# A four-layer graph kernel: counts and tables issued straight behind the lookups, and fp8 stores held to their place in SyncE's queue

## The chip, the cores and the metric

The kernel runs on one NeuronCore of a Trainium2 chip. The metric is the device time in microseconds, the median of several runs. Engines are called TensorE (PE in the profile; its weight loads are PEld), VectorE (DVE), ScalarE (ACT), GpSimd (POOL) and SyncE (SP, which only issues DMAs; its queue is SPq). Each engine works through its own instructions in the order in which they are written down, and the engines wait for each other through semaphores.

## What is computed

There are 16 graphs of 1024 nodes with 128 features each; `adj` holds 0 or 1. Four layers follow each other, each added to its input and normalised:

```python
# layer 0: masked attention over the neighbours
x = layernorm(x + softmax(masked(relu_q @ relu_k.T, adj)) @ relu_v)
# layer 1: for each node the maximum over its neighbours, feature by feature
x = layernorm(x + max_j(relu(p[i] + q[j] + b) * adj[i, j]))
# layer 2: sum over neighbours, then two dense products
x = layernorm(x + where(nodemask, relu(((1 + eps) * x + x_agg) @ W1 + b1) @ W2 + b2, 0))
# layer 3: some edges are removed row after row, each row depending on earlier ones
# ("dilation"); then three rounds of mean over neighbours, dense products, batch norm
x = layernorm(x + graph_sage(x, dilate(adj)))
```

The removal of edges (`_dilate_pattern`) is sequential in the row: the removals of a row also clear the column.

## The kernel before

Most of the time is one stage, `layers_012`, in which layers 0 to 2 and the removal of edges run side by side. Its backbone is the maximum of layer 1. The nodes of a graph are taken in groups of six; for each group a table holds the maxima over all 64 subsets. Two groups make a slot, so a graph has NP = 86 slots, and 16 graphs make 1376. A slot has two half slots `h`, one for each half of the 1024 columns. In a half slot:

- `look_up` (L843) writes `pg` in PSUM with four matmuls: the table's part `high` and its part `low`, each for two groups, times `hot`, a matrix that has a one where a column's subset is the table's. There are two `pg` buffers.
- `count` (L812, L813) prepares `hot` for the slot after the next: a matmul of the fp8 tile `AT` with the constant `lit` into `pm`, and ScalarE's activation of `pm` into `hot`.
- `table` (L824, L827), in every second slot, transposes the tables of two slots ahead on TensorE into `pt` and copies them on ScalarE into `high`; `low_part` (L832, L834), half a slot later, subtracts `high` from `pt` by a matmul and copies the rest into `low`. `pm` and `pt` share two PSUM buffers.
- VectorE takes the maximum of `best` and `pg` into `best` (L908).

All other work of the stage is written as generators ("streams"): attention of the next graph (`scores` with `off` L337 and the exponentials `e` L359; `attend` with the transposes of `e` L387, their copy `eT` L390, the product `pav` L397), the rest of layers 1 and 2 (`rest`), the tables' subset maxima on VectorE (`tables_of`, `sub` L482 and L486) and layer norm. A stream hands over one piece at a time with an engine and an estimated cost. A planner, `advance`, issues in each half slot those pieces for which its budgets (`ROOM`) and its delays allow it, TensorE's first and then the others; mostly a piece that needs another's result is issued half a slot later. The removal of edges is a further generator, `dilation`, asked by `dilate_on` when its due time has come. It works in 32 blocks of 32 rows, one block in about 43 slots. In each, GpSimd goes through 31 steps (L669 to L679), in which it issues what comes due there; VectorE prepares the next block (`prepare`, with the scan `U` L544, its result `V` passed through DRAM, L555 and L556); `hit` goes through DRAM to VectorE (L686, L689, `hit_T` L703); and `remove` ranks edges with TensorE and ScalarE (`pturn` L590, `prank` L599, `rank` L601), finds the edges `gone` on VectorE (L613, two buffers) and stores them from SyncE (L615).

In the half slot the order of issue is: lookups, a piece of `dilation` (before or after the streams), the streams' pieces, `low_part`, `count`, `table`, and last VectorE's maximum. TensorE, ScalarE, VectorE and GpSimd keep this order as written (`manual_schedule`). SyncE isn't among them: the order of its DMAs is made by the scheduler, from its own estimate of when each is ready.

`load_columns` brings in the adjacency. In each graph nine chunks of 120 rows of the transposed adjacency are loaded, by a DMA that GpSimd issues (L764) and that converts to fp8, into `AT`, which has four buffers. The call for chunk `at` also stores chunk `at - 1` from SyncE (L758) into `adj8` in DRAM, which layer 3 reads much later. It is called every ten slots, two chunks ahead of use. SyncE's queue also has the loads of X (L747), the stores of layer 2's result (L466) and all DMAs of the removal of edges that are named above, except for the loads of `E`, `An` and `AT`, which GpSimd issues.

After the stage, from about 5088 us, layer 3 runs: three rounds over 16 graphs with other code, which is not touched here.

Of the kernel before, what the change touches and what calls it, by code (L numbers as in the profile page):

```python
# [39 lines left out]
B, N, D, H2 = 16, 1024, 128, 256  # L40
P = 128
T = N // P
GS = 6
PS = 2 * GS
PC = 10
CH = PC * PS
# [28 lines left out]
def tile_graph_layers(ctx: ExitStack, tc, a, out):  # L75
    nc = tc.nc
# [95 lines left out]
    for b in range(B):  # L172
        q, g = divmod(b, G)
        nc.gpsimd.dma_start(out=half_rows[g * R:(g + 1) * R, :, q],
                            in_=a["nodemask"][b].rearrange("(k r) -> r k", r=R))
# [21 lines left out]
    adj8 = [dram.tile([N, N], F8, name=f"adj8_{b}") for b in range(B)]  # L197
# [39 lines left out]
    def behind(ins, start):  # L237
        for i in nc.cur_bb.bb.instructions[start:]:
            tc.add_manual_dep(i, ins.name, mybir.DependencyInfo(
                mybir.DependencyClass.NoSync, mybir.DependencyReason.SCHED_ONLY), reason="pace")  # L240

    def layers_012():
# [227 lines left out]
        def tables_of(b):  # L470

            if b:
                yield ask("V", 0, urgent=True, after=("tables", b - 1))
            for g0 in range(0, NP, TG):
                n_g = 2 * min(TG, NP - g0)
                yield ask("V", 0.01, same=True, urgent=True, after=("q", b))
                made.append((b, g0))
                yield ask("V", 0.1, same=True, urgent=True, after=("used", *made[-3]) if len(made) > 2 else None)
                qg = qs[b].rearrange("o (g s) -> o g s", s=GS)
                subs[b, g0] = w2.tile([P, TG, P], F32, name="sub", bufs=2)  # L480
                sub = subs[b, g0].rearrange("o t (a s) -> o (t a) s", a=2)
                nc.vector.memset(sub[:, :n_g, 0:1], LOWEST)  # L482
                for k in range(GS):
                    n = 1 << k
                    yield ask("V", 0.06 + n * n_g / 960, same=(n < 8), urgent=True)
                    nc.vector.tensor_max(sub[:, :n_g, n:2 * n], sub[:, :n_g, 0:n],  # L486
                                         qg[:, 2 * g0:2 * g0 + n_g, k:k + 1].to_broadcast([P, n_g, n]))
                happened["sub", b, g0] = now
            happened["tables", b] = now
# [255 lines left out]
        def load_x(b):  # L745
            X[b] = apool.tile([P, T, D], F32, name="X", bufs=3)
            nc.sync.dma_start(out=X[b], in_=x[b].rearrange("(t p) d -> p t d", p=P))  # L747
# [4 lines left out]

        def load_columns(at):
            b, c = divmod(at, T + 1)
            if at:
                before, k = divmod(at - 1, T + 1)
                rows = min(CH, N - k * CH)
                nc.sync.dma_start(out=adj8[before][k * CH:k * CH + rows], in_=AT[at - 1][:rows])  # L758
            if b < B:
                rows = min(CH, N - c * CH)  # L760
                t = AT[at] = apool.tile([CH, N], F8, name="AT", bufs=4)
                if rows < CH:
                    nc.gpsimd.memset(t, 0.0)
                nc.gpsimd.dma_start(out=t[:rows], in_=adjT[b, c * CH:c * CH + rows])  # L764

        An, AT, subs, qs, ps, values, exps, bests, hots, tables = ({} for _ in range(10))
# [8 lines left out]
        def start(stream, first=False):  # L775
            pending[stream] = [next(stream, None), -9]
            streams.insert(0 if first else len(streams), stream)
# [27 lines left out]
        def count(s, h):  # L805

            b, g = divmod(s, NP)
            c, r = divmod(g, PC)
            if h == 0:
                hots[s] = w2.tile([P, N], F32R, name="hot", bufs=3)  # L810
            pm = psum.tile([P, 512], F32, tag="subset", name="pm", bufs=2)
            nc.tensor.matmul(pm, lit[:, r, :], AT[b * (T + 1) + c][:, halves[h]], start=True, stop=True)  # L812
            nc.scalar.activation(hots[s][:, halves[h]], pm, AF.Relu, bias=one_less)  # L813

        def table(s):

            b, g = divmod(s, NP)
            g0 = g - g % TG
            assert ("sub", b, g0) in happened, (s, [(x.__name__, pending[x]) for x in streams], room)
            pt = psum.tile([P, 512], F32, tag="subset", name="pt", bufs=2)[:, :2 * P]  # L820
            if g + 2 - g0 == min(TG, NP - g0):
                happened["used", b, g0] = now
            for k in range(2):
                nc.tensor.matmul(pt[:, k * P:(k + 1) * P], subs[b, g0][:, g - g0 + k, :], ident, is_transpose=True,  # L824
                                 start=(k == 0), stop=(k == 1))
            high = w2.tile([P, 2 * P], F32R, name="high", bufs=2)
            nc.scalar.copy(high, pt)  # L827
            tables[s] = pt, high

        def low_part(s):  # L830
            pt, high = tables[s]
            nc.tensor.matmul(pt, less, high, start=False, stop=True, skip_group_check=True)  # L832
            low = w2.tile([P, 2 * P], F32R, name="low", bufs=2)
            nc.scalar.copy(low, pt)  # L834
            tables[s] = high, low

        def look_up(s, h, pg):

            at = s % 2
            for k, part in enumerate(tables[s - at]):  # L840
                for a in range(2):
                    rows = slice(64 * a, 64 * a + 64)
                    nc.tensor.matmul(pg[:, a], part[rows, at * P:(at + 1) * P], hots[s][rows, halves[h]],  # L843
                                     start=(k == 0), stop=(k == 1))

        def merge(b, h):
            best, s = bests[b], halves[h]
            nc.vector.tensor_max(best[:, 0, s], best[:, 0, s], best[:, 1, s])
# [5 lines left out]
        def dilate_on():  # L854
            nonlocal due, wants_bank
            if due <= now and not (wants_bank and taken >= 2 and given.get(taken - 2, 1e9) > now):
                after, cost, wants_bank = next(dilate, (B * NP, 0, False))
                due += after
                room["V"] -= cost

        def slot(s, last):

            nonlocal now
            now = s
            b, g = divmod(s, NP)
            if s >= 0 and g == 0:
                bests[b] = bests[b - 1] if b else w4.tile([P, 2, N], F32, name="best")
                if b + 1 < B:
                    start(tables_of(b + 1), True)
                    load_x(b + 1)  # L870
                    start(attend(b + 1))
                    start(scores(b + 1))
            if s >= 0 and g % PC == 0 and b * (T + 1) + g // PC + 2 <= B * (T + 1):
                load_columns(b * (T + 1) + g // PC + 2)
            for h in range(2):
                now = s + 0.5 * h
                for e in ROOM:
                    room[e] = min(room[e] + ROOM[e] / 2, ROOM[e] / (2 if e in ("PE", "V") else 1))
                if s >= 0:
                    pg = psum.tile([P, 2, 512], F32, tag="wide", name="pg", bufs=2)  # L880
                    look_up(s, h, pg)
                early = s >= 0 and due < now
                if early:
                    dilate_on()
                advance(("PE",))
                advance(("A", "V", "Pool"))
                if s >= 0 and not early:
                    dilate_on()
                if h == 0 and s % 2 and s + 1 < last:
                    low_part(s + 1)  # L890
                if s + 2 < last:
                    count(s + 2, h)
                    if h and s % 2 == 0:
                        table(s + 2)
                if s >= 0:
                    own = bests[b][:, :, halves[h]]
                    if g == 0:
                        if b:
                            if h:
                                merge(b - 1, h)  # L900
                            total(b - 1, h)
                        nc.vector.tensor_copy(own, pg)
                        if b and h:
                            start(rest(b - 1))
                    else:
                        if g == NP - 1 and h:
                            merge(b, 0)
                        nc.vector.tensor_max(own, own, pg)  # L908
            if s >= 0:
                hots.pop(s)  # L910
# [4 lines left out]
        for at in range(2):  # L915
            load_columns(at)
# [13 lines left out]
        with tc.manual_schedule(engines={mybir.EngineType.PE, mybir.EngineType.Activation, mybir.EngineType.DVE,  # L930
# [13 lines left out]
            last = rest(B - 1)  # L944
# [426 lines left out]
```

## Time and profile before

| what | value |
|---|---|
| median of 3 runs | 6208.64 us (6201.9 to 6210.01) |
| the profiled execution's own time | 6199.75 us |
| its span, first to last instruction | 6198.0 us |
| mean granted TensorE clock | 0.962 |
| busy in the span: TensorE, VectorE, ScalarE, GpSimd | 90%, 79%, 64%, 58% |
| TensorE busy in 142 to 5088 us (the slots) | 4486.93 of 4946 us |
| VectorE, ScalarE, GpSimd busy in the same | 4253.75, 3360.82, 3390.78 us |
| TensorE busy from 5088 us to the end | 1015.75 of 1110 us |

In the lines of the profile, a group of instructions is named by line, engine and operation, then what it writes and what it reads, the shape, and how often it ran; behind the bar stand its total busy time and the mean of one in ns; behind the second bar the time that the engine stood idle before it, and what ended most of that. A line of waits gives who waited for whom, the total in us, how often, and the longest. A line of the timeline gives the start in us, the duration, engine, line and operation, and in brackets the idle time before it with what ended it.

### The profile page before, as it was taken

Reading aid. Unit: us, or ns where it says so; the run is one execution under the profiler, and the core shown is the slowest. Engines: PE = TensorE matmul, PEld = TensorE weight load, DVE = VectorE, ACT = ScalarE, POOL = GpSimd, SP = SyncE. Lnnn points to the kernel's source line nnn. Section 1 sums busy time; section 2 is a strip of 40 time slices with the busy share of each in tenths; the row PEclk is TensorE's granted clock in tenths of the full one; section 3 lists DMA queues with packets and bytes.
Section 4 is the critical chain, followed back from the end, with each engine's and each line's share of the span. In section 5 each row is a group of like instructions: output and inputs, shape, how many; then the busy total and the mean of one; then the engine's idle time right before and its main releaser. Section 6 shows DMA issues by size and latency. Waiting matters only on the chain.

```text
span 6198.0 us, 93287 instructions
## 1 busy us (share of the span) xinstructions
PE 5582.7 (90%) x30144; PEld 3046.0 (49%) x30250; DVE 4870.0 (79%) x7484; ACT 3988.2 (64%) x7362; POOL 3613.1 (58%) x11879
## 2 busy tenths in 40 slices
PE   5989899989898989999989798989999878999998
PEld 4545454545454545454545454545444435555654
DVE  3888788888888888889888788888889875555455
ACT  3767676767676767677767576767666554344855
POOL 2676666667666767677777757667677651110114
PEclk8999999989999999999999899999999989999999
DMA  5021213121212212122121211212121014554645
GB/s 42 11 33 25 40 22 42 22 40 24 40 24 31 32 32 32 32 32 38 26 43 22 39 24 31 31 31 33 31 33 28 19 41 124 159 144 133 214 163 191
DMA packets 496976, 334.28 MB, mean 54 GB/s; under 512 B 303338, under 2 KB 448228, under 8 KB 492388
## 3 DMA queue, kind: packets, MB, share of 16 engines
q1 hardware_dynamic: 405504, 260.29, 14.5%
q0 software_dynamic: 89008, 67.42, 12.6%
q8 instruction: 237, 3.88, 0.3%
q14 instruction: 255, 2.09, 0.1%
q10 hardware_dynamic: 1972, 0.59, 0.1%
HBM read 362.38 MB, written 133.96 MB: 80 GB/s over the span
## 4 chain that ended last, share of the span: by engine, by line
PE 31%; DVE 10%; ACT 4%; POOL 3%; issue 2%; DMA 1%; SPq 0%; DVEq 0%; POOLq 0%; ACTq 0%
PE pg L843 7%; PE pagg L1071 5%; DVE best L908 5%; PE pm L812 3%; PE po L1101 2%; PE po L1095 1%; PE pa L439 1%; PE pav L397 1%; PE pp L300 1%; ACT hot L813 1%; PE pdeg L1026 1%; DVE near L1014 1%; PE psc L349 1%; PE prank L599 1%; PE pe L387 1%
## 5 line engine op out<-in xcount | busy, mean ns | idle before, releaser
L908 DVE TENSOR_TENSOR best<-best,pg 128x1024 f32<-128x1024 f32 x2720 | 3259.3, 1214 | 512.6 <-PE pg L843 501.7
L813 ACT ACTIVATE hot<-pm,one_less 128x512 fp32r<-128x512 f32 x2752 | 1887.4, 689 | 780.5 <-PE pm L812 773.2
L843 PE MATMUL pg<-hot,high 64*128 64x512 f32 x5504 | 1407.3, 508 | 258.9 <-DVE best L908 220.8
L843 PE MATMUL pg<-hot,low 64*128 64x512 f32 x5504 | 1115.5, 402 | 0.0
L812 PE MATMUL pm<-AT,lit 120*128 120x512 fp8e4 x2752 | 1085.9, 395 | 4.5 <-ACT low L834 3.5
L843 PEld LDWEIGHTS pg<-hot,high 64*128 64x128 f32 x5504 | 523.5, 187 | 1014.6 <-DVE best L908 492.8
L669 POOL TENSOR_SCALAR sc<-low_counts,half_mask,rest 16x1 f32<-16x1 f32 x992 | 354.4, 357 | 393.9 <-DVE rest L655 283.2
L843 PEld LDWEIGHTS pg<-hot,low 64*128 64x128 f32 x5504 | 537.9, 192 | 0.0
L812 PEld LDWEIGHTS <-lit 120*128 120x128 fp8e4 x2752 | 270.3, 98 | 389.8 <-issue 313.5
L674 POOL TENSOR_SCALAR sc<-sc 16x1 f32<-16x1 f32 x992 | 393.1, 396 | 105.1
L834 ACT CAST low<-pt 128x256 fp32r<-128x256 f32 x688 | 256.0, 372 | 263.3 <-PE pt L832 261.9
L671 POOL TENSOR_SCALAR sc<-sc 16x1 f32<-16x1 f32 x992 | 324.5, 327 | 107.6
L1116 POOL TENSOR_TENSOR length<-length,mhalf 128x8 f32<-128x8 f32 x48 | 78.9, 1644 | 489.2 <-DVE length L1115 489.2
L676 POOL TENSOR_SCALAR hit<-V,sc 16x31 bf16<-16x31 bf16 (+30 forms) x992 | 362.4, 365 | 0.0
L677 POOL TENSOR_SCALAR last_rank<-V,sc 16x31 f32<-16x31 bf16 (+30 forms) x992 | 342.9, 346 | 0.0
L832 PE MATMUL pt<-high,less 128*128 128x256 f32 x688 | 279.2, 406 | 67.6 <-ACT high L827 61.5
L824 PE MATMUL pt<-ident,sub 128*128 128x128 f32 x1376 | 277.5, 283 | 51.8 <-ACT hot L813 50.0
L486 DVE TENSOR_TENSOR sub<-sub,q 128x24 f32<-128x24 f32 (+11 forms) x768 | 304.0, 397 | 24.8 <-ACT q L304 10.4
L397 PE MATMUL pav<-v,eT 128*128 128x128 f32 x2048 | 301.5, 292 | 2.0 <-ACT eT L390 2.0
L397 PEld LDWEIGHTS pav<-v,eT 128*128 128x128 f32 x2048 | 255.4, 196 | 73.3 <-issue 55.7
L670 POOL TENSOR_SCALAR sc<-sc 16x1 f32<-16x1 f32 x992 | 237.0, 239 | 86.5
L349 PE MATMUL psc<-kT,qT 128*128 128x256 f32 x1024 | 276.3, 388 | 9.9 <-issue 9.9
(270 smaller groups left out, 9662.9 us busy)
## 6 DMA issues: line engine op xcount, KB each, us to landing
removed<-gone SPq DMA_DIRECT2D x128, 256.0 KB
An<-in_adj_dram POOLq DMA_DIRECT2D x16, 1024.0 KB, 16.0
E<-in_adj_dram POOLq DMA_DIRECT2D x128, 128.0 KB, 6.6
gone_all<-removed POOLq DMA_DIRECT2D x64, 256.0 KB, 10.2
near<-adj SPq DMA_DIRECT2D x16, 1024.0 KB
kept<-near SPq DMA_DIRECT2D x16, 1024.0 KB
share<-share SPq DMA_DIRECT2D x32, 512.0 KB
hidden<-r SPq DMA_DIRECT2D x32, 512.0 KB
```

Of the source, the lines that this page charges most:

```text
L349: nc.tensor.matmul(psc[:, 256 * i:256 * (i + 1)], qT[:, t * P:(t + 1) * P], kT[:, s.start + 256 * i:s.start + 256 * (i + 1)], start=False, ...
L397: nc.tensor.matmul(pav, eT[:, c, :], values[b][:, c, :], start=(c == 0), stop=(c == T - 1))
L669: gp.tensor_scalar(half, mine, half_mask[:, m], rest[:, n:n + 1], op0=ALU.mult, op1=ALU.add)
L671: gp.tensor_scalar(sf, half, 5.5, sf, op0=ALU.is_gt, op1=ALU.mult)
L674: gp.tensor_scalar(to, at, sf, none, op0=ALU.subtract, op1=ALU.subtract)
L676: gp.tensor_scalar(hit[:, n, n + 1:], V[:, n, n + 1:], at, None, op0=ALU.is_equal)
L677: gp.tensor_scalar(last[:, n + 1:], V[:, n, n + 1:], to, None, op0=ALU.is_le)
L812: nc.tensor.matmul(pm, lit[:, r, :], AT[b * (T + 1) + c][:, halves[h]], start=True, stop=True)
L813: nc.scalar.activation(hots[s][:, halves[h]], pm, AF.Relu, bias=one_less)
L843: nc.tensor.matmul(pg[:, a], part[rows, at * P:(at + 1) * P], hots[s][rows, halves[h]], start=(k == 0), stop=(k == 1))
L908: nc.vector.tensor_max(own, own, pg)
L1071: nc.tensor.matmul(pa[:, s], piece[:, t, :], m[c][:, s], start=(i == 0), stop=(i == 15))
```

## The change

Two edits are made in `slot` and `load_columns`.

In a half slot `low_part`, `count` and `table` are now issued directly behind `look_up`, ahead of `dilation`'s piece and of the streams' pieces. The planner's decisions are the same, and so is VectorE's maximum at the end of the half slot.

The call of `load_columns` for chunk `at` now stores chunk `at - 2`, and the store is given a dependency for the scheduler alone (no semaphore), which ties it behind the instruction written just before it. `behind` is a helper that was there already. One more call, at slot 80 of the last graph, makes the last store.

```diff
         def load_columns(at):
             b, c = divmod(at, T + 1)
-            if at:
-                before, k = divmod(at - 1, T + 1)
+            if at > 1:
+                before, k = divmod(at - 2, T + 1)
                 rows = min(CH, N - k * CH)
-                nc.sync.dma_start(out=adj8[before][k * CH:k * CH + rows], in_=AT[at - 1][:rows])
+                begin = len(nc.cur_bb.bb.instructions)
+                nc.sync.dma_start(out=adj8[before][k * CH:k * CH + rows], in_=AT[at - 2][:rows])
+                behind(nc.cur_bb.bb.instructions[begin - 1], begin)
...
-            if s >= 0 and g % PC == 0 and b * (T + 1) + g // PC + 2 <= B * (T + 1):
+            if s >= 0 and g % PC == 0:
                 load_columns(b * (T + 1) + g // PC + 2)
             for h in range(2):
...
                     look_up(s, h, pg)
+                if h == 0 and s % 2 and s + 1 < last:
+                    low_part(s + 1)
+                if s + 2 < last:
+                    count(s + 2, h)
+                    if h and s % 2 == 0:
+                        table(s + 2)
                 early = s >= 0 and due < now
                 if early:
                     dilate_on()
...
                 if s >= 0 and not early:
                     dilate_on()
-                if h == 0 and s % 2 and s + 1 < last:
-                    low_part(s + 1)
-                if s + 2 < last:
-                    count(s + 2, h)
-                    if h and s % 2 == 0:
-                        table(s + 2)
                 if s >= 0:
                     own = bests[b][:, :, halves[h]]
```

```python
    def behind(ins, start):
        for i in nc.cur_bb.bb.instructions[start:]:
            tc.add_manual_dep(i, ins.name, mybir.DependencyInfo(
                mybir.DependencyClass.NoSync, mybir.DependencyReason.SCHED_ONLY), reason="pace")
```

## The prediction

> **What bounds the kernel now.** I read the page first: engine shares, then the costliest groups.
>
> ```profile
> PE 5582.7 (90%) x30144; PEld 3046.0 (49%) x30250; DVE 4870.0 (79%) x7484; ACT 3988.2 (64%) x7362; POOL 3613.1 (58%) x11879
> ...
> L908 DVE TENSOR_TENSOR best<-best,pg 128x1024 f32<-128x1024 f32 x2720 | 3259.3, 1214 | 512.6 <-PE pg L843 501.7
> L813 ACT ACTIVATE hot<-pm,one_less 128x512 fp32r<-128x512 f32 x2752 | 1887.4, 689 | 780.5 <-PE pm L812 773.2
> L843 PE MATMUL pg<-hot,high 64*128 64x512 f32 x5504 | 1407.3, 508 | 258.9 <-DVE best L908 220.8
> ```
>
> L908 runs once in each half slot, from about 142 to 5088 us: 4946 us over 2720 half slots is 1.82 us each. The busy times by stretch give TensorE 4487 us of that (91%) and VectorE 4254 us (86%). Two engines this full, coupled through two `pg` buffers: the stage lasts as long as TensorE's work and TensorE's gaps together. The work is the same after the change, so I list the gaps. In the TensorE timeline the gaps between 330 and 4830 us sum to 405 us: 106 us in gaps over 3 us, 299 us in shorter ones. The waits of all engines in that stretch name them:
>
> ```profile
> PE pg L843 <- DVE best L908: 205.6, 272, 16.4
> DVE gone L613 <- DMA removed<-gone: 80.6, 9, 18.0
> PE pt L832 <- ACT high L827: 56.0, 153, 1.5
> ...
> PE ptr L290 <- DMA X<-in_x_dram: 28.7, 4, 20.3
> ...
> PE pt L824 <- ACT hot L813: 24.6, 50, 1.3
> PE pe L387 <- ACT e L359: 17.3, 38, 1.0
> ```
>
> Nine waits of VectorE for a DMA make 80.6 us; that is no load of work but a stall. SyncE's own waits (the DMA queue's) tell where it comes from:
>
> ```profile
> SPq L758 <- DMA AT<-in_adjT_dram: 2473.3, 124, 54.8
> ```
>
> The fp8 stores of line 758 hold SyncE for 2473 us, 20 us at a time, waiting for the load whose tile they store. One such place in the timeline:
>
> ```profile
> 633.45 0.39 PE L812 MATMUL pm<-AT,lit 120*128 120x512 fp8e4 x1
> 642.28 0.65 POOL L764 DMA_DIRECT2D AT<-in_adjT_dram  x1 [0.29 <-POOL AT L763]
> 645.34 0.45 SPq L758 DMA_DIRECT2D adj<-AT  x1
> 645.85 0.58 SPq L615 DMA_DIRECT2D removed<-gone  x1
> ...
> 648.55 0.55 DVE L613 TENSOR_SCALAR gone<-rank,least,match 128x1024 bf16<-128x1024 f16 x1 [18.03 <-DMA removed<-gone]
> ...
> 650.28 0.80 PE L843 MATMUL pg<-hot,high 64*128 64x512 f32 x2 [16.44 <-DVE best L908]
> ```
>
> The store stood in SyncE's queue before GpSimd had issued the load (642.28). Behind it waited the store of an earlier `gone` tile, free only at 648; VectorE, in order, could not write the next `gone`, so `best` came late and TensorE stood 16.44 us. The lookup after it takes 0.80 instead of 0.50 us: TensorE also resumes at a lower clock.
>
> **What the skill says.** "DMA: Bandwidth & Descriptors", Anatomy of one DMA: a DMA's semaphore wait is made by the issuing sequencer before dispatch. The trace agrees: the 2473 us are SyncE's. "TensorE: Matmul & The Clock Gate", What's actually happening: after an idle window of about 3.4 us the array runs at half clock until it has been busy for about as long. The trace agrees in kind (0.80 against 0.50 us, full speed again 6.7 us later, at 657.00). Same page, the detail on queue depths: ScalarE and VectorE are strictly first in, first out, TensorE pulls only weight loads ahead. So a moved piece delays all behind it.
>
> **The change part by part.** Sums are against the profiled execution: 6199.75 us, span 6198.0 plus 1.75. The median shown, 6208.64, is 8.9 above it; I carry the difference over.
>
> *Stores.* A store now belongs to the tile loaded two chunks earlier and is tied to its place. In the built order before, 62 SyncE transfers that VectorE's results feed (54 of `removed`, 8 of V) stand behind a store whose load is issued at a later slot; in the changed build none. The store's wait then ends 10 slots or more (36 us at 3.64 us a slot) after its load was issued, against 3.9 us from issue to landing (median; longest 29.7). So the queue no longer blocks. TensorE's gaps at the nine `gone` stalls are 16.44, 3.93, 8.92, 6.48, 14.86, 9.97, 3.02, 2.96, 3.50 = 70.1 us. The X load was blocked in the same way twice (store at 3548.01, X load at 3548.43, while its last tile was freed by a store at 3524.22): gaps 20.31 and 8.04 = 28.3. Together 98.4 us. Lower clock after them: 21 lookups of over 0.6 us follow these eleven gaps, one per half slot; at 0.50/0.80 of the speed a 1.8 us half slot loses 1.1, so about 20 us. In a stall ScalarE and GpSimd get ahead, and that lead goes: I give back a tenth, 10 us. Three long gaps are not the stores' and stay: 10.6 at 400 and 14.9 at 5032 (GpSimd's rank loop ends late), 8.0 at 4860 (ScalarE behind GpSimd's `left`).
> The later store leaves the tile's buffer free 10 slots before the load that reuses it (four buffers): nothing. The 144 stores are the same number; the last one comes at slot 80 of the last graph, and its rows are read hundreds of us later: nothing.
>
> *Order.* VectorE's and GpSimd's sequences are the same in both builds; only TensorE and ScalarE differ. Before: lookups, streams, counts. Now: lookups, counts, streams. Cyclically the lookups (0.9 us) move from behind the counts to ahead of them, so `hot` comes up to 0.9 us later against the streams' matmuls, and `high` and `low` no longer stand behind the streams' ScalarE pieces. Gain, at most all of L832's and L824's waits: 56.0 + 24.6 = 80.6; at least 0. I take 50, as some waits only give way to `pg`. Loss: `e` (L359) and `off` (L337), 1.14 us each and some 120 times in the stage, now start behind `hot`. In the trace the median time from the end of `e` to its transposes on TensorE is 0.33 us; giving each `e` that directly follows its lookup work the later start and subtracting its own slack gives 28 us, `off` 5; I take 35. At most: 0.9 us for all 240, and 0.4 (one count) for 240 copies to `eT`, 312 us; at least 0. Net -15.
> VectorE's stream pieces may start 0.4 us later against the lookups, but need 0.4 to 0.8 us and have the lookups' 0.9 as cover; where two stand in one half slot up to 0.4 shows. Nothing in the sum, part of the range.
>
> Sum: -98 - 20 + 10 - 15 = -123. 6199.75 - 123 = 6077 for a profiled run; as a median 6208.64 - 123 = **6086**.
>
> **The rivals.**
> *GpSimd takes over the stall.* The rank loop (31 steps of 3.3 us) feeds `hit`, and in about every other block VectorE takes `hit_T` only 6.4 to 8.5 us after the DMA is issued, of which the DMAs need 5.6. If VectorE no longer stops at `gone`, it stops there. Against: in those blocks GpSimd itself waits for VectorE's `U`, 22.0, 10.4 and 16.7 us beside stalls of 18.0, 9.1 and 14.9, and would start earlier by as much. If it happens, only the X gaps and the order remain: 28 + 15, 6166 us.
> *ScalarE becomes late (slower).* In strict order a stream's long piece now waits for counts that wait for lookups. It decides from a loss of 158 us (98 + 20 - 10 + 50), half of the upper bound 312. Halfway from there to the bound, 235, gives 6208.6 + 77 = 6286. Against: ScalarE is 68% busy in the stage, and the slacks measured give 33.
> *Short waits for VectorE go too.* Of 205.6 us of `pg` waits 138 are short ones; with steadier `hot` and `low` half could go: 6086 - 69 = 6017. Against: nothing in VectorE's order changes.
> *It doesn't do what it says*: stores still hoisted and the order's two sides equal: 6209. The built order excludes the first half.
>
> **Chances.** Forecast 0.62 (own range 6045 to 6130: loss or gain of the order up to 40 more, give-back 0 to 30), GpSimd 0.12, ScalarE slower 0.08, short waits 0.13, no change 0.02, the order's loss just near 158 0.03. About 0.2% (12 us) is what can be told from no change. Faster 0.62 + 0.12 + 0.13 = 0.87; same 0.05; slower 0.08. The range 6030 to 6170 takes in the forecast, GpSimd's case and half of the short-waits case; left out are 0.08 + 0.05 + 0.07 = 0.20.
>
> **What would show it.** Stores: SyncE's wait for AT falls from 2473 us to under 200, VectorE's wait for `removed<-gone` and TensorE's for X to about nothing; if instead `hit_T<-hit_p` appears nine times, it is GpSimd. Order: L832's and L824's waits fall from 80 to about 30, `pe<-e` rises from 17 to about 45; if TensorE's waits for `e`, `off`, `eT` exceed 150 us, the slower rival holds. I am wrong if the `removed` waits vanish and the time falls by less than 60 us: then the gaps were not on the path.

## The result, and the profile after

The changed kernel takes 6129.59 us (median of 4 runs, 6125.1 to 6140.09) against 6207.42 us (4 runs, 6201.9 to 6210.01): a ratio of 0.9878 with the interval 0.9861 to 0.9895, or 78 us less. The forecast was 123 us less. The direction and the range held, but the result lies at the very edge of the forecast's own range (6045 to 6130): 45 us of the forecast gain are missing, and most of the experiments look for them.

The profiled execution takes 6132.99 us, with a span of 6131.2 us and a mean granted clock of 0.968 (0.962 before). From its page, the engines' shares and the groups shown of before:

```profile
PE 5574.5 (91%) x30145; PEld 3063.1 (50%) x30250; DVE 4869.7 (79%) x7484; ACT 3986.5 (65%) x7362; POOL 3647.4 (59%) x11879
...
L910 DVE TENSOR_TENSOR best<-best,pg 128x1024 f32<-128x1024 f32 x2720 | 3257.5, 1214 | 472.4 <-PE pg L845 462.6
L815 ACT ACTIVATE hot<-pm,one_less 128x512 fp32r<-128x512 f32 x2752 | 1890.0, 688 | 1061.8 <-PE pm L814 1052.0
```

The work is the same as before; only the idle times differ. (The new lines shift the code by two, so L910 is the former L908, and so on.) VectorE stands 40 us less ahead of its maximum. ScalarE stands 281 us more ahead of `hot`: its `hot` now comes early in its order and waits there for `pm`, and what stands behind it waits along. It doesn't idle more in all, since its busy time is the same and the span is shorter; ahead of `eT`, for example, it stood 54.6 us between 330 and 4830 us before and stands 8.9 now. Its idle time has moved ahead of `hot`.

The waits of all engines between 330 and 4830 us, the stretch used before:

```profile
PE pg L845 <- DVE best L910: 182.6, 307, 13.9
...
PE pe L387 <- ACT e L359: 58.9, 74, 2.0
PE pt L834 <- ACT high L829: 44.8, 132, 9.9
DVE e L352 <- PE psc L349: 37.6, 57, 1.3
POOL counts L546 <- DVE U L544: 27.4, 11, 6.4
...
PE pt L826 <- ACT hot L815: 13.1, 29, 0.8
DVE hit_T L703 <- DMA hit_p<-hit: 12.5, 1, 12.5
```

In the kernel before, three of these groups had, in the same stretch:

```profile
POOL counts L546 <- DVE U L544: 119.2, 13, 22.0
...
DVE e L352 <- PE psc L349: 13.9, 30, 0.9
...
DVE hit_T L703 <- DMA hit_p<-hit: 9.3, 1, 9.3
```

The nine waits of VectorE for `removed<-gone` (80.6 us) and TensorE's waits for an X load (28.7 us) are no longer there. GpSimd's waits for `U` fell from 119.2 to 27.4 us, and `hit_T` is waited for once, as before. TensorE's waits for `e` rose from 17.3 to 58.9 us. And its waits for `best`, 205.6 us before, fell by only 23, though seven of the nine stalls, 57 us, stood in that line.

Of SyncE's own waits in that stretch those for `AT`, which had 2473.3 us, are down to a single one of 34.2. The first two lines of the list and this one:

```profile
SPq L615 <- DVE gone L613: 1756.4, 110, 55.9
SPq L686 <- POOL hit L678: 640.9, 23, 51.8
...
SPq L759 <- DMA AT<-in_adjT_dram: 34.2, 1, 34.2
```

SyncE waits for work that VectorE and GpSimd haven't done yet, hardly ever for a load. SyncE's timeline at the place shown in the prediction:

```profile
636.02 0.33 SPq L615 DMA_DIRECT2D removed<-gone  x1
...
641.31 2.24 SPq L759 DMA_DIRECT2D adj<-AT  x1
654.35 0.32 SPq L615 DMA_DIRECT2D removed<-gone  x1
```

The fp8 store stands between two stores of `gone` and holds up neither.

To see where the time went, I laid TensorE's records of the profiled executions end to end, from the first to the last maximum of VectorE. Each gap is put down to the releaser that the timeline names; one of more than 2.5 us is "long". All in us; what lies at the ends of the stage, 2 to 3 us, is left out:

| kernel | stage | TensorE busy | long gaps | short gaps | of the short: `best` | `high` and `hot` | `e` and `off` | issue at `psc`, `prank` |
|---|---|---|---|---|---|---|---|---|
| before | 4945.3 | 4486.4 | 131.9 | 324.7 | 169.2 | 87.4 | 25.3 | 17.3 |
| after | 4875.1 | 4473.1 | 43.4 | 355.9 | 198.1 | 52.4 | 73.7 | 0.2 |
| stores_alone | 4838.8 | 4474.5 | 39.1 | 322.9 | 165.2 | 88.0 | 25.2 | 17.3 |
| order_alone | 5018.2 | 4512.1 | 156.4 | 347.1 | 190.6 | 53.6 | 70.1 | 0.7 |
| e_and_off_first | 4829.6 | 4481.9 | 37.4 | 307.7 | 202.3 | 70.6 | 2.9 | 0 |
| e_first_old | 4821.1 | 4489.6 | 30.3 | 298.9 | 193.9 | 66.9 | 9.7 | 0 |
| tensor_more | 4885.5 | 4550.8 | 35.3 | 297.0 | 141.5 | 80.7 | 23.1 | 26 |
| vector_more | 4845.5 | 4465.9 | 36.8 | 340.7 | 185.0 | 85.3 | 23.2 | 17 |

The last column is no waiting. Some matmul records are missing from these traces: in before, of 256 matmuls `psc<-off` and 1024 `prank` there are 195 and 979; in after, stores_alone, order_alone and vector_more it is the same to one; in tensor_more 192 and 926; in e_and_off_first and e_first_old none is missing. An "issue" gap stands where such a matmul ran. Two places of the timeline of before, one with the record and one without:

```profile
826.35 0.40 PE L843 MATMUL pg<-hot,low 64*128 64x512 f32 x2
826.68 0.39 PE L348 MATMUL psc<-off,penalty 128*128 128x512 bf16 x1
826.90 1.03 PE L349 MATMUL psc<-kT,qT 128*128 128x256 f32 x4
...
830.08 0.39 PE L843 MATMUL pg<-hot,low 64*128 64x512 f32 x2
830.63 1.03 PE L349 MATMUL psc<-kT,qT 128*128 128x256 f32 x4 [0.16 <-issue]
```

From the lookup to `psc<-kT` it is 0.55 us in both. (In after and order_alone such a matmul stands behind other matmuls than a lookup, and most of these gaps, of some 0.06 us, are too short to be named.) So the last column belongs to the work, and from here on "work" is the sum of it and of the busy time, and "waits" are the other short gaps.

The stage is 70.2 us shorter: long gaps -88.5, work -30.4, waits +48.3. The rest of the run is 3.5 us longer. So the stalls went as forecast, and the waits took back more than half of it.

### The profile page after: what moved, and what is told of

It reads as the page before. It is cut to its first block, busy times and chain, and to the rows that moved or that the text cites. A ratio compares the mean times of both kernels' runs of the same rounds, so it can differ in the third digit from the quotient of the medians.

```text
span 6131.2 us, 93265 instructions
## 1 busy us (share of the span) xinstructions
PE 5574.5 (91%) x30145; PEld 3063.1 (50%) x30250; DVE 4869.7 (79%) x7484; ACT 3986.5 (65%) x7362; POOL 3647.4 (59%) x11879
## 4 chain that ended last, share of the span: by engine, by line
PE 60%; DVE 22%; ACT 10%; issue 4%; POOL 3%; DMA 1%; SPq 0%; DVEq 0%; ACTq 0%; POOLq 0%
PE pg L845 18%; DVE best L910 12%; PE pm L814 8%; PE pagg L1073 5%; PE pav L397 3%; ACT hot L815 3%; PE psc L349 3%; PE pa L439 3%; PE pp L300 2%; PE pt L834 2%; DVE sub L486 2%; PE pe L387 2%; PE prank L599 2%; ACT e L359 2%; PE po L1103 2%
## 5 line engine op out<-in xcount | busy, mean ns | idle before, releaser
L910 DVE TENSOR_TENSOR best<-best,pg 128x1024 f32<-128x1024 f32 x2720 | 3257.5, 1214 | 472.4 <-PE pg L845 462.6
L674 POOL TENSOR_SCALAR sc<-sc 16x1 f32<-16x1 f32 x992 | 408.2, 412 | 104.8
L671 POOL TENSOR_SCALAR sc<-sc 16x1 f32<-16x1 f32 x992 | 321.4, 324 | 107.5
L834 PE MATMUL pt<-high,less 128*128 128x256 f32 x688 | 269.7, 392 | 54.1 <-ACT high L829 49.7
L834 PEld LDWEIGHTS pt<-high,less 128*128 128x128 f32 x688 | 130.3, 189 | 326.1 <-ACT high L829 204.9
L670 POOL TENSOR_SCALAR sc<-sc 16x1 f32<-16x1 f32 x992 | 237.5, 239 | 86.6
L826 PE MATMUL pt<-ident,sub 128*128 128x128 f32 x1376 | 275.1, 282 | 14.4 <-ACT hot L815 13.5
L397 PE MATMUL pav<-v,eT 128*128 128x128 f32 x2048 | 281.8, 282 | 2.1 <-ACT eT L390 2.1
L1052 ACT CAST m<-near 128x1024 fp32r<-128x1024 fp8e4 x256 | 249.3, 1050 | 48.2 <-PE pagg L1073 48.2
```

Of the source, the lines that this page charges most:

```text
L397: nc.tensor.matmul(pav, eT[:, c, :], values[b][:, c, :], start=(c == 0), stop=(c == T - 1))
L671: gp.tensor_scalar(sf, half, 5.5, sf, op0=ALU.is_gt, op1=ALU.mult)
L674: gp.tensor_scalar(to, at, sf, none, op0=ALU.subtract, op1=ALU.subtract)
```

## The experiments

The theory after the result: the stores bring nearly all of the gain, and the new order costs time, because the exponentials `e` now stand behind `hot` on ScalarE. Its rivals: the order gains as forecast and the stores bring less than forecast; or the order's loss comes through VectorE, whose pieces start later.

**stores_alone**: the stores of the changed kernel with the half slot of the kernel before.

```diff
...
-                nc.sync.dma_start(out=adj8[before][k * CH:k * CH + rows], in_=AT[at - 1][:rows])
+                begin = len(nc.cur_bb.bb.instructions)
+                nc.sync.dma_start(out=adj8[before][k * CH:k * CH + rows], in_=AT[at - 2][:rows])
+                behind(nc.cur_bb.bb.instructions[begin - 1], begin)
```

> The changed stores alone, half slot in the old order. Theory A (the stores give the whole gain and the new order costs): the eleven long TensorE gaps (98 us) and the lower clock after them (13 us in the trace of the changed kernel) go, the short gaps of the stage stay at about 325 us instead of 356: 6207 - 105 = about 6100, some 30 us faster than the changed kernel. Theory B (the order gains a little, as forecast, and the stores gave less than forecast): slower than the changed kernel, 6140 or more, with long gaps left or short ones grown at VectorE's waits.

Measured: 6090.03 us, ratio 0.9821 (0.9805 to 0.9837): 112 us less, and the interval lies wholly below that of the changed kernel. The waits between 330 and 4700 us:

```profile
PE pg L845 <- DVE best L910: 144.3, 256, 10.8
...
PE pt L834 <- ACT high L829: 56.1, 154, 1.5
...
PE pt L826 <- ACT hot L815: 24.6, 50, 1.3
```

The short waits are as they were before; only the stalls are gone. On top of these stores, the other half of the change is therefore a loss.

**order_alone**: the half slot of the changed kernel with the stores of the kernel before.

```diff
+                if h == 0 and s % 2 and s + 1 < last:
+                    low_part(s + 1)
+                if s + 2 < last:
+                    count(s + 2, h)
...
                 advance(("PE",))
...
```

> The new half slot order alone, stores as before. Theory A: the nine waits for the store of gone and the two for X remain, TensorE's waits for e rise from 18 to some 60 us and its short waits for best by some 30, those for high and hot fall by 35: 6207 + 30 = about 6238. Theory B: the waits for high and hot fall and little else rises: 6190.

Measured: 6267.08 us, ratio 1.0108 (1.0093 to 1.0123), 65 us more: the right sign, and more than expected. Its waits between 330 and 4700 us:

```profile
DVE gone L613 <- DMA removed<-gone: 85.6, 9, 17.9
...
PE pe L387 <- ACT e L359: 54.5, 73, 2.0
...
PE ptr L290 <- DMA X<-in_x_dram: 43.2, 3, 19.0
```

The stalls are all there, and `e` is late as in the changed kernel. By the table, 39 of its 73 us in the stage are waits; 25 are long gaps, most of it one more stall for X (17.0 us at 3283), and 9 are work, with a clock of 0.954 against 0.962. So the two halves don't simply add up: 112 us less and 65 more, against 78 less for both.

**lag1_tied** and **lag2_untied** take the two parts of the store's edit apart, in the old half slot. Shown is what differs from stores_alone.

```diff
...
-                nc.sync.dma_start(out=adj8[before][k * CH:k * CH + rows], in_=AT[at - 2][:rows])
+                nc.sync.dma_start(out=adj8[before][k * CH:k * CH + rows], in_=AT[at - 1][:rows])
                 behind(nc.cur_bb.bb.instructions[begin - 1], begin)
```

> Old order; the store is tied to its place, but is still that of the chunk loaded last (one chunk back, as before). If the place in SyncE's queue is what counts (theory A), a load issued ten slots earlier has landed and this equals stores_alone, about 6100. If the second chunk of delay is needed, stores still wait for late loads: some of the 98 us remain, 6120 to 6200.

```diff
                 nc.sync.dma_start(out=adj8[before][k * CH:k * CH + rows], in_=AT[at - 2][:rows])
-                behind(nc.cur_bb.bb.instructions[begin - 1], begin)
```

> Old order; the store is that of two chunks back, but without the tie. In the built order 68 transfers of the removal of edges still stand behind a store whose load is issued later. Theory A: the stalls remain, about 6207. If the delay by a chunk is what counts: about 6100.

Measured: with the tie and the former lag 6103.23 us, ratio 0.9844 (0.9827 to 0.9861), an interval that overlaps that of stores_alone; with the longer lag and no tie 6204.22 us, ratio 1.0001 (0.9988 to 1.0014). In the first, SyncE's waits for `AT` between 330 and 4700 us are down to 72.7 us. In the second they are as before (between 330 and 4830 us):

```profile
SPq L758 <- DMA AT<-in_adjT_dram: 2482.7, 124, 55.1
```

There 68 of SyncE's transfers stand in the built order behind a store whose load comes later (62 before). The tie does nearly all of it, 99 of the 112 us. A store of an older tile is hoisted just the same.

**copies_late**: the changed kernel, with ScalarE's copies `hot`, `high` and `low` put back behind the streams' pieces, so that only TensorE's order is new.

```diff
-            nc.scalar.activation(hots[s][:, halves[h]], pm, AF.Relu, bias=one_less)
+            copies.append(lambda: nc.scalar.activation(hots[s][:, halves[h]], pm, AF.Relu, bias=one_less))
...
+                for copy in copies:
+                    copy()
```

> The changed kernel, but ScalarE's part of low_part, count and table (the copies to low, hot and high) stands behind the streams' pieces, as before; TensorE keeps the new order. Theory V (the new TensorE order itself makes VectorE's stream pieces late, since the streams' matmuls now end right before the lookups): TensorE's waits for e fall back from 64 to about 18 us, but its short waits for best stay near 198 us and VectorE's waits for psc and pav near 38 and 15 us; waits for high and hot come back, 60 and 27 us or more. Time 6090 + 33 to 6090 + 70, so 6125 to 6160. Theory E (late exponentials are the cause, and the waits for best follow from them): the waits for best fall back to about 165 us too, and the time to about 6095.

Measured: 6371.02 us, ratio 1.0254 (1.0231 to 1.0277). Between 330 and 4700 us:

```profile
PE pt L836 <- ACT high L831: 192.7, 293, 2.1
...
PE pg L847 <- DVE best L915: 126.5, 231, 2.6
PE pt L828 <- ACT hot L817: 80.5, 193, 1.5
```

The `e` waits are gone (4.1 us), but TensorE now waits far longer for the copies that its own order asks for early. All expected times were missed: here TensorE's order could not be changed without ScalarE's. This run doesn't price the late `e`.

**e_and_off_first**: the changed kernel, with the exponentials and `off` (the pieces with these estimated costs) issued on ScalarE straight behind the lookups, ahead of `low`, `hot` and `high`. `advance` got an argument that restricts it to pieces of the given costs.

```diff
                     look_up(s, h, pg)
+                advance(("A",), (1.05, 1.1))
                 if h == 0 and s % 2 and s + 1 < last:
```

> The changed kernel, but ScalarE's pieces e and off, which need nothing of the same half slot, are issued straight behind the lookups, ahead of low_part, count and table (the planner takes them first, so other pieces may move by half a slot). Theory V: TensorE's waits for e fall from 64 to under 25 us, the waits for best stay near 198 us: 6129 - 40 = about 6090. Theory E: both fall: 6129 - 75 = about 6055.

Measured: 6079.77 us (6072.4 to 6085.12), ratio 0.9778 (0.976 to 0.9797): about 50 us less than the changed kernel, and less than both kernels. Between 330 and 4700 us:

```profile
PE pg L845 <- DVE best L911: 174.9, 296, 7.9
...
PE pt L834 <- ACT high L829: 43.7, 147, 1.7
...
PE pe L387 <- ACT e L359: 2.9, 4, 1.4
```

TensorE's waits for `e` are 2.9 us here, against 58.9. But the waits for `best` stay at 174.9 us, 31 above stores_alone. By the table, against stores_alone, 40 us of TensorE's waits for `high`, `hot`, `e` and `off` went and 37 came back at `best`, so this kernel is hardly better than stores_alone. How much of the gain over the changed kernel is owed to the late `e` alone, e_first_old below tells.

**tables_early**: only `low_part` and `table` early, `count` late, on the new stores.

```diff
-                if s + 2 < last:
-                    count(s + 2, h)
-                    if h and s % 2 == 0:
-                        table(s + 2)
+                if s + 2 < last and h and s % 2 == 0:
+                    table(s + 2)
...
                 advance(("A", "V", "Pool"))
+                if s + 2 < last:
+                    count(s + 2, h)
```

> Stores as changed; only low_part and table stand behind the lookups, count stays behind the streams as before. Theory V: the matmuls of count still separate the streams' matmuls from the next lookups, so the waits for best stay at 165 us; high has half a slot more and its waits fall from 61 us to under 15, those for hot before a table from 27 to under 10; e starts later by one copy of 0.37 us in every fourth half slot, at most 10 us; some waits of count for the PSUM buffer of low may come, 10 to 20 us. 6090 - 60 + 25 = about 6055, faster than both kernels. Theory E: high and low stand ahead of e on ScalarE here too, waits for e and best rise by 15 us and more: 6080.

Measured: 6119.86 us, ratio 0.9843 (0.9826 to 0.986); 6055 was expected. TensorE's waits for `high` are gone, but `pm` now waits for `hot`, 55.8 us between 330 and 4700, through the shared two buffers, and TensorE's busy time in the stage is 50 us longer than in stores_alone:

```profile
PE pm L814 <- ACT hot L815: 55.8, 101, 1.6
```

Of the 50 us, 34 are the table's transposes, 308 against 283 ns on average. The other 17 or so are no loss: no record is missing in this trace, and they stand in the last column of the table for stores_alone.

**e_first_old**: the same call for `e` and `off` on stores_alone, that is in the old order. If the waits for `best` come from VectorE's pieces standing in a worse place in the new order, they should not rise here.

```diff
                     look_up(s, h, pg)
+                advance(("A",), (1.05, 1.1))
                 early = s >= 0 and due < now
```

> stores_alone (old half slot order) with ScalarE's pieces e and off issued straight behind the lookups: the control for e_and_off_first. If that kernel's lead of 10 us over stores_alone comes from e and off alone, this one gains the 25 us of waits for e and off: about 6065, faster than e_and_off_first. If the new order has a gain of its own once e isn't late, this stays at or above 6080.

Measured: 6078.35 us (6068.66 to 6084.36), ratio 0.9794 (0.9777 to 0.9811). Between 330 and 4700 us:

```profile
DVE best L911 <- PE pg L845: 415.7, 761, 2.9
...
PE pg L845 <- DVE best L911: 166.9, 299, 6.1
...
DVE e L352 <- PE psc L349: 7.6, 18, 0.5
```

VectorE's own waits for `psc` are 7.6 us and for `pav` 4 us, so its pieces are not late, and the waits for `best` rise all the same, from 144.3 to 166.9 us. The theory of the misplaced pieces isn't needed for that rise. And the new order is worth nothing by itself: with `e` and `off` ahead, old order and new order take the same time.

The same run prices the late `e`. In the old order, where `e` isn't late, the edit still shortens the stage by 18 us, in the new order by 46. So about 28 of the 36 us that the new order costs go away with it. As the edit may also move other pieces by half a slot, that is the price of the late `e` and `off` so far as these four kernels can tell it.

**maximum_first** and **maximum_first_old** move VectorE's maximum ahead of the dilation's and the streams' pieces, the first on e_and_off_first, the second on stores_alone.

```diff
-                advance(("PE",))
-                advance(("A", "V", "Pool"))
...
                     own = bests[b][:, :, halves[h]]
...
+                advance(("PE",))
+                advance(("A", "V", "Pool"))
```

> e_and_off_first with one more edit: VectorE's maximum stands ahead of the streams' VectorE pieces of the same half slot, so each such piece has the length of a maximum (1.2 us) more after the streams' matmuls it reads. Theory V (VectorE's pieces wait for streams' matmuls that the new order puts right before the lookups, and hold up the maximum): VectorE's waits for psc and pav fall from 39 to under 10 us, TensorE's short waits for best from 202 to 165 us or less: 6080 - 37 = about 6045, if no other wait for VectorE's pieces comes in. Theory W (the waits for best are only what VectorE's own load of 87% leaves, whatever stands where; the waits that went elsewhere turn up here): waits for best stay near 200 us, 6080.

> The same edit on stores_alone, the old half slot order. Theory V: only 18 us of such VectorE waits are there to go: waits for best 165 to about 150 us, 6090 - 15 = 6075. Theory W: 6090.

Measured: 6273.38 us, ratio 1.0109 (1.009 to 1.0129), and 6372.0 us, ratio 1.0263 (1.0245 to 1.0282). Both missed by far. In the first, between 330 and 4700 us:

```profile
DVE best L904 <- PE pg L845: 589.5, 848, 3.8
```

VectorE stood 381.4 us ahead of the maximum in e_and_off_first; here 589.5. The lookups are not ready when VectorE comes to the maximum, and the pieces that could have filled the time are behind it. In these two kernels the streams' pieces ahead of the maximum were cover, not an obstacle. The edit also changed other waits, so it doesn't decide between the two theories.

**vector_more** and **tensor_more** load one engine, on stores_alone: a small memset on VectorE in each half slot, and a second, quarter-wide matmul into `pm`, which the full one overwrites.

```diff
+                    nc.vector.memset(extra_v, 0.0)
```

> stores_alone with one memset of 64 columns more on VectorE in each half slot, ahead of the maximum: about 0.07 us each by the memset of sub (62 to 78 ns), 2752 of them, about 190 us of VectorE's time. Theory W (VectorE is nearly as much the limit as TensorE; what TensorE saves elsewhere comes back in good part as waits for best): half or more of it shows, 6090 + 95 to 6090 + 190, so 6185 to 6280, with waits for best rising by as much. Theory V (the waits for best come from pieces that stand in the wrong place, and VectorE has room: it waits some 417 us for lookups): under a fifth shows, below 6130.

```diff
+            nc.tensor.matmul(pm[:, :128], lit[:, r, :], columns[:, :128], start=True, stop=True)
             nc.tensor.matmul(pm, lit[:, r, :], columns, start=True, stop=True)
```

> stores_alone with a second, quarter-wide matmul of count (128 of 512 columns, with its weight load) in each half slot, which writes nothing that is kept: about 0.06 to 0.15 us each, 2752 of them, 165 to 410 us of TensorE's time. Theory W: more than half, but not all of it shows, since waits for best shrink by 40 us or more while TensorE is busy: waits for best fall from 165 to under 125 us. Theory V: all of it shows and the waits for best stay near 165 us.

Measured: vector_more 6103.87 us, ratio 0.9843 (0.9825 to 0.9861), tensor_more 6137.78 us, ratio 0.9895 (0.988 to 0.991). VectorE's busy time in the stage grew by about 105 us, and the stage by 7 (the medians differ by 14, and the intervals overlap). VectorE's idle time ahead of the maximum took nearly all of it; between 330 and 4700 us it is 416.8 us in stores_alone, and in vector_more:

```profile
DVE best L912 <- PE pg L846: 321.6, 577, 3.1
```

So VectorE doesn't set the length on a level with TensorE. TensorE's work grew by 85 us (165 to 410 were expected, a figure without a source), the stage by 47: its waits for `best` shrank from 165 to 142 us, the others and the long gaps by some 15.

## Why the prediction was right, and where it wasn't

**What bounds it.** Reading the stage as TensorE's work plus its gaps was right. That the table's columns add up to the stage shows nothing, since work and gaps of any engine do; what shows it is that added work on TensorE costs 47 of 85 us, and on VectorE 7 to 14 of 105.

**Stores: right, the sum in part by luck.** Forecast -98 -20 +10 = -108 us; stores_alone gave -106.5 in the stage and -112 in the median. The eleven stalls of 98 us are all gone. The other two terms are less sure:

- The give-back of 10 us. The three long gaps that were to stay are there in stores_alone, 6 us longer in all. In the changed kernel they are 13.91 us at 401, 9.87 at 4785 and 19.66 at 4957, against 10.6, 8.0 and 14.9: just the 10 us. But in order_alone, which keeps all stalls, the same three are 8 us longer too. So the equality with the forecast is luck, and a lead lost with the stalls is not shown to be the cause.
- The clock's 20 us. TensorE's busy time fell by 12, but that can't be told from the scatter between profiles of the same work: it is 4487 and 4498 us with the stalls (before, lag2_untied), 4475 and 4499 without (stores_alone, lag1_tied).

One point of the reasoning was too generous: the age of the stored tile, ten slots or more, was given as the reason why the queue no longer blocks. The tie alone gives nearly all of it, the age alone nothing.

**Order: the step that failed.** The forecast was "gain 50, loss 35, net -15". On top of the stores it measured +36 in the stage. By the table, after against stores_alone:

- The gain was too large, and most of it came back. The waits for `high` and `hot`, the term of the 50 us, fell by 36. The forecast allowed that "some waits only give way to `pg`", but put nothing in the sum for it beyond the step from 80.6 to 50; the waits for `best` rose by 33 us.
- The loss by `e` and `off`, taken as 28 and 5, is +45 and +3. The working gave the later start to "each `e` that directly follows its lookup work" and to no other. Told apart in the traces by what stands between `e` and the last `hot` on ScalarE: for the 78 of 128 `e` with nothing there, or only `high` or `low`, TensorE's waits rise from 4.8 to 33.5 us, 29 as against the 28 forecast. For the 50 behind a further piece they rise from 14 to 31, and these had been given nothing. One of them in the timeline of the changed kernel, with VectorE's `top`, the last that this `e` needs:

```profile
622.04 0.21 DVE L356 TENSOR_SCALAR top<-tops 128x1 f32<-128x1 f32 x1
...
623.59 0.69 ACT L815 ACTIVATE hot<-pm,one_less 128x512 fp32r<-128x512 f32 x1 [0.73 <-PE pm L814]
...
624.18 0.36 ACT L829 CAST high<-pt 128x256 fp32r<-128x256 f32 x1
...
624.43 0.60 ACT L591 CAST ET<-pturn 128x512 bf16<-128x512 f32 x1
...
624.91 1.17 ACT L359 ACTIVATE e<-e,top 128x1024 f32<-128x1024 f32 x1
...
626.22 0.66 PE L387 MATMUL pe<-ident,e 128*128 128x128 f32 x4 [0.53 <-ACT e L359]
```

  ScalarE stands 0.73 us at `hot` while `e` could run, then does `hot`, `high` and a copy of the removal of edges, which would stand ahead of `e` in the old order too, and only then `e`; TensorE stands 0.53 us at the transposes of `e`. A delay of `hot` passes through the pieces between.
- "VectorE's stream pieces ... Nothing in the sum" held as far as it goes: VectorE's waits for `psc` rose from 13.9 to 37.6 us, but e_first_old has nearly the same rise of the `best` waits without them.

In sum: `high` and `hot` -36, `best` +33, `e` and `off` +48, smaller waits +4, long gaps +4, work -18: +36. The 18 us of work are less than the 24 by which lag1_tied and stores_alone differ in busy time, so no cause is named for them.

**That the waits come back is measured, not explained.** In e_first_old 37 us of TensorE's waits for `high`, `hot`, `e` and `off` went and 29 came back as waits for `best`; in e_and_off_first 40 and 37; in tensor_more 85 us of work were added and 24 of these waits went. It fits a TensorE that, with fewer delays, meets VectorE's maximum more often, since there are only two `pg` buffers between them. That is argued. In the changed kernel it doesn't fit by itself: there the other waits rose by 13 in all, and those for `best` rose too. The runs show that the rise needs no misplaced pieces, and exclude a VectorE that limits as strongly as TensorE; a kernel with a third `pg` buffer would tell more, and wasn't tried.

**The rivals.** GpSimd did not take over the stall: there is one wait for `hit_T`, as before, and GpSimd's wait for `U` fell by 92 us, which is the lead that was named against this rival. ScalarE did become late, by the mechanism described, at 48 us instead of the 158 from which it decides. The short waits for VectorE did not go; they rose. The tell-tales: SyncE's wait for `AT` and both kinds of stall went as said; L834's and L826's waits fell to 58 us, not 30 (48 without a gap of 9.9 us at 4785, whose counterpart before lay outside the stretch); `pe<-e` rose to 59, not 45.

## What to carry to other kernels

A store that a scheduler places in a shared in-order DMA queue is worth checking against the load it waits for: here its place alone cost 99 us, and its age nothing. When a piece is moved ahead on an in-order engine, price everything that then stands behind it, also what follows only at second hand, and look for the one long operation (here `e`) that should go ahead of it. Of waits that are removed on an engine coupled by two buffers to one nearly as full, don't count on the whole: here 29 of 37 and 37 of 40 us came back. And before an idle time called "issue" is counted as a wait, see whether a record is missing there.

## What the runs showed of the hardware

A small operation beside a large one cost VectorE far less than its record. The memset's record is 112 ns (70 were expected), 308 us in all, but the busy time grew by 105 us: with it the maximum's mean fell from 1213 to 1183 ns, some 80 us in all, and the records overlap each other by 120 us more.

```profile
L912 DVE TENSOR_TENSOR best<-best,pg 128x1024 f32<-128x1024 f32 x2720 | 3213.1, 1183 | 386.5 <-PE pg L846 366.7
L899 DVE MEMSET extra_v<- 128x64 f32 x2749 | 307.9, 112 | 0.0
```

On TensorE a matmul of 128 columns has a record of 227 ns, 624 us in all, and added 76 us of busy time, or 85 of work. Here overlap isn't the only reason. With the added work TensorE was granted a higher clock: 0.979 to 0.981 in the four runs of tensor_more, against 0.966 to 0.971 in those of stores_alone and of vector_more, and the two kinds of lookup took 501 and 396 ns on average instead of 507 and 402. So in these two runs a record's mean, times the count, was an upper bound of what an operation added to the busy time.
